# 64x64 tiles for a product of layer 1, and an earlier place for f, g and h of the second image in layer 2

## The chip, the cores and the metric

One core of one Trainium2 chip runs the whole kernel as a single program. The metric is the device time of that program in microseconds (us), the median of several executions. A trace by the hardware profiler gives one further execution in detail. Engines are named as in the profile: PE (TensorE matmuls; PEld are its weight loads), DVE (VectorE), ACT (ScalarE), POOL (GpSimd), SP (SyncE, which here issues DMAs).

## The reference

Four layers follow each other on x of shape (2, 512, 32, 32) in fp32, that is two images of 512 channels and 1024 pixels. Layer 0 is a deformable attention with a learned position bias and an MLP; the change does not touch it. The rest, cut to what matters:

```python
# layer 1: linear attention, 8 heads of d = 64 channels
K = conv1x1(X, Wq, bq); Q = conv1x1(X, Wk, bk); V = conv1x1(X, Wv, bv)   # each as (b, head, d, n)
M = einsum('bhmn,bhen->bhme', K, V)
Out = einsum('bhme,bhmn->bhen', M, Q)
Out = conv1x1(Out, Wo, bo) + X            # then a batch norm over both images, with gamma and beta
# layer 2: non-local attention, mid = 128
f = relu(bn_eval(conv1x1(x, wf, bf), ...)); g = relu(bn_eval(conv1x1(x, wg, bg), ...))
h = conv1x1(x, wh, bh)
attn = softmax(einsum('bcn,bcm->bnm', f, g) * mid ** -0.5)                 # 1024 x 1024 for each image
x = conv1x1(einsum('bnm,bcm->bcn', attn, h), wv, bv) + x
# layer 3: theta, phi and g have one channel each
y = softmax(theta[:, :, None] * phi[:, None, :]) @ g
x = sigmoid(se2(relu(se1(mean(x))))) * bn(W_w * y + W_b) + x
```

## The kernel before

The program is written in one function over tile pools. A scheduler orders the instructions of each engine by what they wait for, so the order in the text is not the order on the engine, except where an instruction is pinned (`keep_in_program_order`: in layer 0, and in `last` near the end). Channels lie on the 128 partitions in four blocks (`KC = 4`); an image is 1024 columns (`HW`). PSUM, where PE writes, has eight banks of 128x512 fp32 that the pools hand out; a pool's `bufs` says how many tiles of a tag can be open at once, and the next tile waits until the readers of an earlier one are done.

**Layer 1** never forms K, Q and V. It makes each image's Gram matrix G = X X' (L1357), and from it U = G Wv, M = Wq U (per head), R = M Wk and A = R Wo, all of 512x512, and at last the output from A and X. The products with 512 on every side go through `seven` (L1314 to L1334), a Strassen-like scheme: seven products of blocks instead of eight, each two matmuls of 128x256 columns on PE, with sums and differences on DVE. The eight heads of M lie on the diagonal: for block `o` the tile `M[b][:, o]` is 128x128, holds heads 2o and 2o+1 as two 64x64 blocks, and is zero beside them (the memset of L1441). The matmuls of M (L1447) already write 64 rows each; DVE adds the bias term to each block (L1457).

R is made per image and block by one 128x512 matmul (`prk`, L1472) into a one-bank PSUM tile of the pool `dpg` (tag "g", four buffers), which DVE (even blocks) or ACT (odd blocks) copies to SBUF (L1473). Beside it, small matmuls (`prb`, L1475) multiply M with the bias of Wk into the pool `dps` (tag "ps", four buffers). `weights_of(R[b])` then makes three working differences and one sum of R's blocks (S1, S2, S3, S4) on DVE, and `moving_of(wot)` those of the transposed Wo once. `seven` with R starts with a product that needs only R itself; its second product needs S2.

**Layers 2 and 3** run image by image from four functions. `l2_fg` (L1629) makes f and g: 16 matmuls (`pf2`) of 512 columns, evicted by four activations on ACT. `l2_h` (L1650) makes one of eight pixel blocks of h: four matmuls (`ph2`) of 128 columns, and one addition on DVE. `l2_attn` (L1662) goes through eight row blocks t: two matmuls into `pscore` (two banks, L1667), the row maximum on DVE (L1678), the exponential on ACT (L1681), reciprocal and scaling on DVE, eight transposes on PE (`pt2`, L1687) and two copies on ACT (L1688) into `at2`. Its argument `between` is called once for each t and puts other work between. `l2_out` (L1691) does 16 matmuls `pz` (L1696) that sum over all of `at2` and `ht`, eight matmuls `pr2` (L1707), and adds the result to x.

Layer 3 of image 0 is `l3_scores` (L1719): rows of theta, phi and g (`prow`, L1728), spread to all partitions (`pp3`, copied to `pg` in SBUF by ACT, L1750), extremes on DVE; it returns `part(t)` (L1774), one exponential of 128x1024 on ACT (L1776) and one weighting on DVE (L1784), for t = 0 to 7, on three buffers `e3`. `l3_out` (L1790) ends image 0 and stores it by four DMAs. For image 1 all of `l2_out` and layer 3 is in `last` (L1839), pinned in its order, and stores by eight DMAs.

The order of these is set at the end of the program (L2039 to L2058). Image 0's f, g, h, attention and `l2_out` use PSUM pools `fp1` (three one-bank buffers, tag "ps") and `fph` (one buffer, tag "h"), beside `fps` (two `pscore` of two banks each). Then these two pools close, and `fp2` (two buffers) and `gps` (one of two banks, tag "l3") open:

```python
nd, part = l3_scores(0, gp, gps)
fg = l2_fg(1, fp, ps)
ht = fp.tile([P, 8, MID], F32, name="ht")
for t in range(8):
    l2_h(1, t, ht, ps, "ps")
    if t % 2:
        part(t // 2)
at2 = l2_attn(1, fp, fps, ps, fg, lambda t: part(4 + t // 2) if t % 2 else None)
l3_out(0, gp, gps, nd)
```

So image 1's f, g and h come after image 0's `l3_scores`, four of the `part` go between the blocks of h, and four between the row blocks of the attention.

Of the kernel before, what the change touches and what calls it, by code (L numbers as in the profile page):

```python
# [10 lines left out]
F32 = mybir.dt.float32  # L11
# [5 lines left out]
P = 128  # L17
B, C, H, W = 2, 512, 32, 32
HW = H * W
NT = B * HW  # L20
KC = C // P
TK = 8
DH = 64
# [4 lines left out]
MID = C // 4  # L28
# [44 lines left out]
def conv_seq(  # L73
# [22 lines left out]
    nc = tc.nc  # L96
# [40 lines left out]
    with ExitStack() as ctx_l0:  # L137
# [264 lines left out]
        with tc.tile_pool(name="a", bufs=1) as a, tc.tile_pool(name="apk", bufs=1, space=PSUM) as apk, tc.tile_pool(  # L402
            name="apc", bufs=1, space=PSUM
# [13 lines left out]
            for t in (0, 2, 1, 3):  # L417
                b, half = divmod(t, 2)
# [136 lines left out]
            for i, (ky, kx) in enumerate(taps_pe):  # L555
# [4 lines left out]
                        lhsT=diag[:, i, :],  # L560
                        rhs=qg[:, ch.g, yi, r, c_, xi],
                        start=(i == 0),
                        stop=(i == len(taps_pe) - 1),
# [72 lines left out]
        with tc.tile_pool(name="hid", bufs=3) as hid, tc.tile_pool(name="sm", bufs=1) as sm, tc.tile_pool(name="hps", bufs=2, space=PSUM) as hps, tc.tile_pool(  # L636
            name="sps", bufs=1, space=PSUM
# [451 lines left out]
        for t in range(NT // 512):  # L1089
            ts_ = slice(t * 512, (t + 1) * 512)  # L1090
            for o in range(KC):
                po = mh.tile([P, 512], F32, name="po")
                for k in range(KC):
                    nc.tensor.matmul(  # L1094
                        po,
                        lhsT=(vwo, wo)[t // 2][:, k, o * P : (o + 1) * P],
                        rhs=q[:, k, ts_],
                        start=(k == 0),
                        stop=(k == KC - 1),
# [46 lines left out]
    with ctx_w:  # L1146
        with tc.tile_pool(name="mo", bufs=2, space=PSUM) as mo, tc.tile_pool(name="m", bufs=3) as m, tc.tile_pool(name="mv", bufs=1) as mv:
# [22 lines left out]
            hs = {}  # L1170
# [106 lines left out]
    with tc.tile_pool(name="d", bufs=2) as d, tc.tile_pool(name="dpg", bufs=4, space=PSUM) as dpg, tc.tile_pool(  # L1277
        name="dps", bufs=4, space=PSUM
    ) as dps:
        both = range(B)  # L1280
        wq, wv, wk, wot, won = (lw[:, i] for i in range(5))
# [3 lines left out]
        G, U, M, R, A, bias1 = {}, {}, {}, {}, {}, {}  # L1285
# [55 lines left out]
        for b in both:  # L1341
# [3 lines left out]
            for t in range(8):  # L1345
# [10 lines left out]
                for i in range(KC):  # L1356
                    nc.tensor.matmul(  # L1357
                        pgs[i],
                        lhsT=xt[:, i * P : (i + 1) * P],
# [78 lines left out]
        for b in both:  # L1438
# [4 lines left out]
            for o in range(KC):  # L1443
# [11 lines left out]
                for h in range(2):  # L1455
# [7 lines left out]
                        ALU.add,  # L1463
                    )
        rblocks, prbs = {}, {}
        for b in both:
            R[b] = d.tile([P, KC, C], F32, name="R", tag="G")
            prb = prbs[b] = dps.tile([P, C], F32, name="prb", tag="ps")
            for o in range(KC):
                mo_ = M[b][:, o].rearrange("p h e -> p (h e)")  # L1470
                pr = dpg.tile([P, C], F32, name="prk", tag="g")
                nc.tensor.matmul(pr, lhsT=mo_, rhs=wk[:, o, :], start=True, stop=True)  # L1472
                (nc.vector.tensor_copy, nc.scalar.copy)[o % 2](R[b][:, o, :], pr)  # L1473

                nc.tensor.matmul(  # L1475
                    prb[:, o * P : (o + 1) * P],
                    lhsT=v("L1_conv_bk", o).to_broadcast([P, P]),
                    rhs=mo_,
                    start=True,
                    stop=True,  # L1480
                )
            rblocks[b], steps = weights_of(R[b])
            for step in steps:
                step()
            if b == 0:
                wotblocks, steps = moving_of(wot)
                for step in steps:
                    step()
# [140 lines left out]
    def l2_fg(b, fp, ps):  # L1629
        fg = fp.tile([P, 2, HW], F32, name="fg")  # L1630
        for i, half in ((0, 0), (0, 1), (1, 0), (1, 1)):
            pf = ps.tile([P, 512], F32, name="pf2", tag="ps")
            for j, k in enumerate((0, 2, 3, 1)):
                nc.tensor.matmul(
                    pf,
                    lhsT=l2w[:, k, i, :],
                    rhs=x[:, k, b * HW + half * 512 : b * HW + (half + 1) * 512],
                    start=(j == 0),
                    stop=(j == KC - 1),
                )  # L1640
            nc.scalar.activation(
                fg[:, i, half * 512 : (half + 1) * 512],
                pf,
                AF.Relu,
                bias=l2s[:, 1, 1:2] if i else l2f[:, 1:2],
                scale=l2s[:, 0, 1:2] if i else l2f[:, 0:1],
            )
        return fg

    def l2_h(b, t, ht, ps, tag):  # L1650
        ph = ps.tile([P, MID], F32, name="ph2", tag=tag)
        for k in range(KC):
            nc.tensor.matmul(
                ph,
                lhsT=x[:, k, b * HW + t * P : b * HW + (t + 1) * P],
                rhs=l2w[:, k, 2, :],
                start=(k == 0),
                stop=(k == KC - 1),
            )
        nc.vector.tensor_tensor(ht[:, t, :], ph, rowb[:, C : C + MID], ALU.add)  # L1660

    def l2_attn(b, fp, fps, ps, fg, between=None):  # L1662
        at2 = fp.tile([P, 8, HW], F32, name="at2", bufs=1)
        for t in range(8):
            pscore = fps.tile([P, 2, 512], F32, name="pscore")
            for half in range(2):
                nc.tensor.matmul(  # L1667
                    pscore[:, half, :],
                    lhsT=fg[:, 0, t * P : (t + 1) * P],
                    rhs=fg[:, 1, half * 512 : (half + 1) * 512],  # L1670
                    start=True,
                    stop=True,
                )
            if between is not None:
                between(t)
            psf = pscore.rearrange("p a n -> p (a n)")
            nm = fp.tile([P, 1], F32, name="nm")
            nc.vector.tensor_reduce(nm, psf, AX.X, ALU.max, negate=True)  # L1678
            e2 = fp.tile([P, HW], F32, name="e2")
            den = fp.tile([P, 1], F32, name="den2")  # L1680
            nc.scalar.activation(e2, psf, AF.Exp, bias=nm, accum_out=den)  # L1681
            nc.vector.reciprocal(den, den)
            nc.vector.tensor_scalar(e2, e2, den, None, ALU.mult)
            for mg in range(2):
                pt = ps.tile([P, 4, P], F32, name="pt2", tag="ps")
                for i in range(4):
                    nc.tensor.transpose(pt[:, i, :], e2[:, (mg * 4 + i) * P : (mg * 4 + i + 1) * P], ident)  # L1687
                nc.scalar.copy(at2[:, mg * 4 : mg * 4 + 4, t * P : (t + 1) * P], pt)  # L1688
        return at2

    def l2_out(b, fp, ps, at2, ht):  # L1691
        z = fp.tile([P, HW], F32, name="z")
        for half in range(2):
            pz = ps.tile([P, 512], F32, name="pz", tag="ps")
            for t in range(8):
                nc.tensor.matmul(  # L1696
                    pz,
                    lhsT=ht[:, t, :],
                    rhs=at2[:, t, half * 512 : (half + 1) * 512],
                    start=(t == 0),  # L1700
                    stop=(t == 7),
                )
            nc.scalar.copy(z[:, half * 512 : (half + 1) * 512], pz)
        for half in range(2):
            for o in range(KC):
                pr = ps.tile([P, 512], F32, name="pr2", tag="ps")
                nc.tensor.matmul(  # L1707
                    pr,
                    lhsT=l2wv[:, o * P : (o + 1) * P],
                    rhs=z[:, half * 512 : (half + 1) * 512],  # L1710
                    start=True,
                    stop=True,
                )
                xs = x[:, o, b * HW + half * 512 : b * HW + (half + 1) * 512]
                nc.vector.scalar_tensor_tensor(
                    xs, pr, v("L2_conv_bv", o), xs, ALU.add, ALU.add, accum_out=xavg[:, o, b, half : half + 1]
                )
# [319 lines left out]
    with tc.tile_pool(name="f", bufs=2) as fp, tc.tile_pool(name="g", bufs=1) as gp:  # L2037
        with tc.tile_pool(name="fps", bufs=2, space=PSUM) as fps:
            with tc.tile_pool(name="fp1", bufs=3, space=PSUM) as ps, tc.tile_pool(  # L2039
                name="fph", bufs=1, space=PSUM  # L2040
            ) as psh:
                fg = l2_fg(0, fp, ps)
                ht = fp.tile([P, 8, MID], F32, name="ht")
                at2 = l2_attn(0, fp, fps, ps, fg, lambda t: l2_h(0, t, ht, psh, "h"))
                l2_out(0, fp, ps, at2, ht)
            with tc.tile_pool(name="fp2", bufs=2, space=PSUM) as ps:
                with tc.tile_pool(name="gps", bufs=1, space=PSUM) as gps:
                    nd, part = l3_scores(0, gp, gps)
                    fg = l2_fg(1, fp, ps)
                    ht = fp.tile([P, 8, MID], F32, name="ht")  # L2050
                    for t in range(8):
                        l2_h(1, t, ht, ps, "ps")
                        if t % 2:
                            part(t // 2)
                    at2 = l2_attn(1, fp, fps, ps, fg, lambda t: part(4 + t // 2) if t % 2 else None)
                    l3_out(0, gp, gps, nd)
                with tc.tile_pool(name="gpl", bufs=2, space=PSUM) as gps:
                    last(1, fp, gp, fps, ps, gps, at2, ht)  # L2058
# [126 lines left out]
```

## Time and profile before

| what | us |
|---|---|
| median of 3 executions (lowest to highest) | 2659.73 (2659.29 to 2660.62) |
| the profiled execution | 2659.86 |
| its span, first to last instruction | 2658.1 |

The mean TensorE clock granted over the profiled execution was 0.995 of full speed. By stages of that execution:

| stage | from, to | length | PE busy | DVE busy | ACT busy | PE clock |
|---|---|---|---|---|---|---|
| layer 0, position bias | 0 to 1789 | 1789 | 1771.89 | 1741.04 | 1331.63 | 1.00 |
| layer 0, rest of it and first part of the MLP | 1789 to 2090 | 301 | 300.14 | 185.46 | 98.81 | 1.00 |
| layer 0, MLP | 2090 to 2320 | 230 | 229.98 | 118.89 | 30.83 | 1.00 |
| layer 1, G and U | 2320 to 2395.1 | 75.1 | 72.91 | 39.95 | 8.87 | 1.00 |
| layer 1, M and R | 2395.1 to 2409.1 | 14.0 | shown below | | | |
| layer 1, A | 2409.1 to 2433.9 | 24.8 | shown below | | | |
| layer 1, output | 2433.9 to 2481.8 | 47.9 | 47.90 | 38.39 | 3.92 | 1.00 |
| norm, layer 2 of image 0: f, g, h, attention | 2481.8 to 2530.1 | 48.3 | 44.02 | 25.04 | 23.33 | 0.98 |
| `l2_out` of image 0 | 2530.1 to 2551.5 | 21.4 | 21.40 | 5.23 | 1.76 | 0.96 |
| layer 3 of image 0, layer 2 of image 1 | 2551.5 to 2606.1 | 54.6 | shown below | | | |
| `last`: rest of image 1 | 2606.1 to 2658.1 | 52.0 | 34.10 | 30.25 | 17.60 | 0.80 |

The three rows left open are printed with the prediction. Busy times are sums over the instructions in a stage. A PE that is busy for the whole of a stage says that no other engine held it up there, not that each matmul ran at its best. The last column is the mean clock that the throttle granted to PE in the stage. In the lines below, "PE L1687 MATMUL pt<-cst,e 128*128 128x128 f32 x8" is eight matmuls of line 1687 that write `pt` (names are cut short), on a tile of 128*128 of the array, with an output of 128 partitions x 128 columns; the numbers ahead are start and length in us, and a bracket behind gives the idle time before and what ended it.

### The profile page before, as it was taken

Reading aid. Unit: us, or ns where it says so; the run is one execution under the profiler, and the core shown is the slowest. Engines: PE = TensorE matmul, PEld = TensorE weight load, DVE = VectorE, ACT = ScalarE, POOL = GpSimd, SP = SyncE. Lnnn points to the kernel's source line nnn. Section 1 sums busy time; section 2 is a strip of 40 time slices with the busy share of each in tenths; the row PEclk is TensorE's granted clock in tenths of the full one; section 3 lists DMA queues with packets and bytes.
Section 4 is the critical chain, followed back from the end, with each engine's and each line's share of the span. In section 5 each row is a group of like instructions: output and inputs, shape, how many; then the busy total and the mean of one; then the engine's idle time right before and its main releaser. Section 6 shows DMA issues by size and latency. Waiting matters only on the chain.

```text
span 2658.1 us, 48935 instructions
## 1 busy us (share of the span) xinstructions
PE 2613.7 (98%) x19658; PEld 970.8 (37%) x19658; DVE 2249.6 (85%) x2036; ACT 1557.1 (59%) x2138; POOL 889.2 (33%) x1049
## 2 busy tenths in 40 slices
PE   8999999999999999999999999999999999999997
PEld 4332323233332333333233333323444444476544
DVE  8999999999999999999999999999554444648645
ACT  6776787777678777767867777777221111011334
POOL 2444444444444454444444445444200000000001
PEclk9999999999999999999999999999999999999998
DMA  6888888888888888888989898888410000010001
GB/s 219 162 180 172 161 162 160 170 161 179 169 161 159 162 173 159 181 169 162 176 164 174 159 183 171 157 176 162 97 31 24 16 24 24 27 53 1 0 1 64
DMA packets 114003, 339.23 MB, mean 128 GB/s; under 512 B 22736, under 2 KB 32464, under 8 KB 112496
## 3 DMA queue, kind: packets, MB, share of 16 engines
q0 software_dynamic: 77824, 251.72, 53.0%
q1 hardware_dynamic: 35520, 84.10, 9.6%
q8 instruction: 155, 2.54, 0.4%
q14 instruction: 72, 0.59, 0.1%
q10 hardware_dynamic: 432, 0.28, 0.0%
HBM read 63.12 MB, written 4.46 MB: 25 GB/s over the span
## 4 chain that ended last, share of the span: by engine, by line
PE 90%; DVE 4%; ACT 3%; issue 2%; DMA 1%; POOL 0%; DVEq 0%; ACTq 0%
PE ph L658 61%; PE A L1159 4%; PE D L1159 4%; PE C L1159 4%; PE po L1094 2%; PE B L1159 2%; PE pg L1357 1%; DVE h L390 1%; ACT r L667 1%; DVE r L673 1%; PE pscore L1667 1%; DMA r<-r 1%; PE psim L701 1%; PE pz L1696 1%; PE pt L1687 1%
## 5 line engine op out<-in xcount | busy, mean ns | idle before, releaser
L658 PE MATMUL ph<-h,w2a 128*32 128x512 f32 x16384 | 1772.1, 592 | 10.3 <-ACT r L667 7.5
L667 ACT ACTIVATE r<-ph,sb 128x1024 f32<-128x1024 f32 x1024 | 1141.6, 1115 | 467.8 <-PE ph L658 444.4
L390 DVE CUSTOM_DVE_ANT_1 h<-tab 128x2048 f32<-128x2048 f32 x512 | 1170.5, 2286 | 19.2 <-PE ph L658 16.4
L658 PEld LDWEIGHTS ph<-h,w2a 128*32 128x32 f32 x16384 | 520.9, 109 | 1238.4 <-issue 768.9
L673 DVE SCALAR_TENSOR_TENSOR r<-r,rel,r 128x1024 f32<-128x1024 f32 x512 | 655.1, 1279 | 25.9 <-ACT r L667 24.5
L681 POOL DMA_DIRECT2D r<-r x512 | 474.7, 1142 | 170.8 <-DMA r<-r 160.7
L676 POOL DMA_DIRECT2D r<-r x256 | 234.4, 916 | 733.2 <-DVE r L673 621.9
L692 POOL DMA_DIRECT2D xs<-r x256 | 320.3, 1251 | 103.6 <-DMA xs<-r 97.8
L1441 POOL MEMSET M<- 128x512 f32 x2 | 1.0, 525 | 428.7 <-PE pt L1348 428.7
L176 ACT ACTIVATE tab<-tab,vec 128x256 f32<-128x256 f32 x252 | 137.6, 546 | 0.0
L1952 POOL TENSOR_TENSOR x<-x,aff 128x512 f32<-128x512 f32 x7 | 7.0, 1036 | 318.0 <-ACT e L1917 318.0
L1199 ACT COPY u<-A 128x512 f32<-128x512 f32 x16 | 9.4, 586 | 146.8 <-PE A L1159 146.8
L1178 ACT ACTIVATE h<-h,vec 128x512 f32<-128x512 f32 x32 | 23.1, 721 | 113.5 <-DVE h L1181 113.5
L1181 DVE TENSOR_TENSOR h<-C,u 128x512 f32<-128x512 f32 x32 | 22.1, 691 | 48.5 <-PE C L1159 48.2
L1159 PE MATMUL A<-xn,w 128*128 128x512 f32 x128 | 60.3, 593 | 0.8 <-DVE x L1101 0.8
L1159 PE MATMUL C<-hT,w 128*128 128x512 f32 x128 | 60.3, 592 | 0.0
L1159 PE MATMUL A<-h,w 128*128 128x512 f32 x128 | 60.1, 592 | 0.0
L1219 DVE TENSOR_TENSOR x<-D,x 128x512 f32<-128x512 f32 x32 | 22.1, 692 | 26.0 <-PE D L1159 26.0
L1219 DVE TENSOR_TENSOR x<-C,x 128x512 f32<-128x512 f32 x32 | 22.1, 691 | 24.8 <-PE C L1159 24.8
L892 ACT ACTIVATE e<-e,den 128x64 f32<-128x64 f32 x128 | 42.3, 341 | 0.5 <-DVE den L888 0.5
L878 ACT ACTIVATE e<-psm,mx 128x64 f32<-128x64 f32 x128 | 39.4, 314 | 2.4 <-DVE mx L873 2.3
L1357 PE MATMUL pg<-xt 128*128 128x512 f32 (+3 forms) x128 | 36.4, 439 | 1.4 <-ACT xt L1355 1.1
(411 smaller groups left out, 1918.1 us busy)
## 6 DMA issues: line engine op xcount, KB each, us to landing
r<-r POOLq DMA_DIRECT2D x256, 512.0 KB, 5.0
r<-r POOLq DMA_DIRECT2D x256, 256.0 KB, 5.9
r<-r POOLq DMA_DIRECT2D x256, 128.0 KB, 4.7
tab<-fd SPq DMA_DIRECT2D x63, 512.0 KB, 6.4
xs<-r SPq DMA_DIRECT2D x256, 64.0 KB, 2.7
xs<-r POOLq DMA_DIRECT2D x256, 64.0 KB, 5.5
lw<-in_l_w_dram SPq DMA_DIRECT2D x5, 1024.0 KB, 9.0
x<-in_x_pos_dram SPq DMA_DIRECT2D x4, 1024.0 KB, 17.9
```

The lines of the kernel that those rows point to most:

```text
L176: return nc.scalar.activation(tf, tf if src is None else src[:, :, ax, :], AF.Identity, bias=0.0 if ax == 0 else v("L0_conv_cpb_b1"), scal ...
L390: nc.vector._custom_dve(TENSOR_ADD_SAT, out=h1, in0=columns.unsqueeze(1).to_broadcast([P, 32, 2, 32]), in1=rows_.unsqueeze(3).to_broadcast ...
L658: nc.tensor.matmul(ph[t * 32 : (t + 1) * 32, i, :], lhsT=w2a[:, o], rhs=h1s[2 * p + i][:, half * 16 : (half + 1) * 16, h, :], start=True, ...
L667: pin(nc.scalar.activation(r, ph, AF.Relu, bias=sb3[:, o, 1:2]))
L673: pin(nc.vector.scalar_tensor_tensor(r0, r1, rel[:, i : i + 1], r0, ALU.mult, ALU.add))
L676: pin(nc.gpsimd.dma_start(rs[p, 0], rs.pop((p, 2)), accum_op=ALU.add))
L681: pin(nc.gpsimd.dma_start(r[0 :: 2 * step], r[step :: 2 * step], accum_op=ALU.add))
L692: pin(nc.gpsimd.dma_start(xs_[t][d::8], rs.pop((p, 0))[4::8], accum_op=ALU.add))
L1094: nc.tensor.matmul(po, lhsT=(vwo, wo)[t // 2][:, k, o * P : (o + 1) * P], rhs=q[:, k, ts_], start=(k == 0), stop=(k == KC - 1),)
L1159: nc.tensor.matmul(banks[bank], lhsT=a[an][k], rhs=b_[bn_][k], start=(i < 4 and k == 0), stop=(k == n - 1), skip_group_check=True,)
L1219: nc.vector.tensor_tensor(to, t, to, ALU.add)
L1357: nc.tensor.matmul(pgs[i], lhsT=xt[:, i * P : (i + 1) * P], rhs=xt[:, i * P :], start=(t == 0), stop=(t == 7),)
```

## The change

It has two parts, both of order and tiling. What is computed stays.

**R.** The loop over images and blocks becomes a loop over blocks that serves both images. For each block `o` four matmuls of 64 rows and 512 columns take the four 64x64 blocks of M (image 0 and 1, head 2o and 2o+1) with the matching 64 rows of Wk. Each contracts over 64 partitions (`hs`) and writes 64 partitions of PSUM, so each uses one quarter of the array: for image 0 rows and columns of the same half, for image 1 the output goes to the other half (`half(h ^ b)`), which makes the four quarters different. Image 0's tile is copied as before by one copy, on DVE for even and ACT for odd blocks. Image 1's halves stand exchanged in PSUM and are copied by two copies of 64 partitions each, one on ACT (h = 0) and one on DVE (h = 1). The bias matmuls `prb` move behind this loop and read the same M.

**f, g and h of image 1.** `l2_fg(1)` moves ahead of `l2_out(0)`, and all eight `l2_h(1)` behind it, inside image 0's PSUM pools; the h take the one-buffer tag "h". `l3_scores(0)` comes after them. All eight `part` of image 0's layer 3 are handed to image 1's attention as its `between`, one for each row block, where before there were four between the h and four in the attention.

```diff
         rblocks, prbs = {}, {}
+
+        def half(h):
+            return slice(h * DH, (h + 1) * DH)
+
         for b in both:
             R[b] = d.tile([P, KC, C], F32, name="R", tag="G")
+        for o in range(KC):
+            prk = [dpg.tile([P, C], F32, name="prk", tag="g") for b in both]
+            for b, h in ((0, 0), (0, 1), (1, 0), (1, 1)):
+                hs = half(h)
+                nc.tensor.matmul(
+                    prk[b][half(h ^ b)], lhsT=M[b][hs, o, h, :], rhs=wk[hs, o, :], start=True, stop=True
+                )
+            (nc.vector.tensor_copy, nc.scalar.copy)[o % 2](R[0][:, o, :], prk[0])
+            for h in range(2):
+                (nc.scalar.copy, nc.vector.tensor_copy)[h](R[1][half(h), o, :], prk[1][half(h ^ 1)])
+        for b in both:
             prb = prbs[b] = dps.tile([P, C], F32, name="prb", tag="ps")
             for o in range(KC):
-                mo_ = M[b][:, o].rearrange("p h e -> p (h e)")
-                pr = dpg.tile([P, C], F32, name="prk", tag="g")
-                nc.tensor.matmul(pr, lhsT=mo_, rhs=wk[:, o, :], start=True, stop=True)
-                (nc.vector.tensor_copy, nc.scalar.copy)[o % 2](R[b][:, o, :], pr)
-
                 nc.tensor.matmul(
                     prb[:, o * P : (o + 1) * P],
                     lhsT=v("L1_conv_bk", o).to_broadcast([P, P]),
-                    rhs=mo_,
+                    rhs=M[b][:, o].rearrange("p h e -> p (h e)"),
                     start=True,
                     stop=True,
                 )
...
                 at2 = l2_attn(0, fp, fps, ps, fg, lambda t: l2_h(0, t, ht, psh, "h"))
+                fg = l2_fg(1, fp, ps)
                 l2_out(0, fp, ps, at2, ht)
+                ht = fp.tile([P, 8, MID], F32, name="ht")
+                for t in range(8):
+                    l2_h(1, t, ht, psh, "h")
             with tc.tile_pool(name="fp2", bufs=2, space=PSUM) as ps:
                 with tc.tile_pool(name="gps", bufs=1, space=PSUM) as gps:
                     nd, part = l3_scores(0, gp, gps)
-                    fg = l2_fg(1, fp, ps)
-                    ht = fp.tile([P, 8, MID], F32, name="ht")
-                    for t in range(8):
-                        l2_h(1, t, ht, ps, "ps")
-                        if t % 2:
-                            part(t // 2)
-                    at2 = l2_attn(1, fp, fps, ps, fg, lambda t: part(4 + t // 2) if t % 2 else None)
+                    at2 = l2_attn(1, fp, fps, ps, fg, part)
                     l3_out(0, gp, gps, nd)
                 with tc.tile_pool(name="gpl", bufs=2, space=PSUM) as gps:
                     last(1, fp, gp, fps, ps, gps, at2, ht)
```

In the order that the scheduler gives the changed program, the first seven of image 1's 32 h matmuls stand on PE between image 0's last scores and its last transposes, then f and g, then `pz` and `pr2` of image 0, then the other h matmuls among image 1's scores. On ACT, the first five of image 1's eight attention exponentials come before the first of `part`, the sixth behind six of `part`, the seventh behind seven, and the last behind all eight.

## The prediction

> **What bounds the kernel now.** First the chain of waits that ended last:
>
> ```profile
> PE 90%; DVE 4%; ACT 3%; issue 2%; DMA 1%; POOL 0%; DVEq 0%; ACTq 0%
> ```
>
> TensorE's own work is the chain. So the question is whether PE gets less to do, or idles less, where the change acts. Next, stages by window (columns: length, then busy time and instructions of PE, PEld, DVE, ACT, POOL; PE clock; DMA):
>
> ```profile
> 2395.10:2409.10 14.00, 13.72 (x161) 8.86 (x161) 12.93 (x29) 2.25 (x4) 0.00 (x0) 1.00 0.01 1
> 2409.10:2433.90 24.80, 24.75 (x115) 21.34 (x115) 19.11 (x48) 4.15 (x10) 0.00 (x0) 1.00 0.00 1
> 2551.50:2606.10 54.60, 52.86 (x257) 31.18 (x257) 33.33 (x72) 33.97 (x59) 0.00 (x0) 1.00 0.00 1
> ```
>
> The first row holds M and the products R, the second their use in `seven`, the third runs from the end of `l2_out(0)` to the start of `last`. PE is full in all three. But DVE is busy 12.93 of 14.00 in the first, so a PE saving there meets DVE at once.
>
> Third, the two things about PE itself that decide the prices: a 64x64 group that the kernel already runs, and its idle gap at the end of image 0's attention.
>
> ```profile
> 15.97 1.09 PE L468 MATMUL pq<-xn,qws 64*64 64x512 f32 x8
> 16.99 0.66 PE L257 MATMUL pf<-acc,offw 128*128 128x64 f32 x4
> ...
> 2528.33 1.94 PE L1687 MATMUL pt<-cst,e 128*128 128x128 f32 x8 [2.74 <-DVE e L1683]
> 2530.06 14.71 PE L1696 MATMUL pz<-at,ht 128*128 128x512 f32 x32
> ```
> ```profile
> 2525.70:2528.30 2.60, 0.00 (x0) 0.00 (x1) 1.37 (x4) 1.21 (x2) 0.00 (x0) 0.99 0.00 0
> 2528.30:2531.70 3.40, 3.37 (x10) 2.44 (x11) 0.00 (x0) 1.17 (x2) 0.00 (x0) 0.50 0.02 5
> 2531.70:2533.40 1.70, 1.70 (x5) 0.76 (x4) 0.00 (x0) 0.00 (x0) 0.00 (x0) 1.00 0.00 0
> ```
>
> The trace counts two passes for each fp32 matmul. Passes of 512 columns elsewhere start 0.429 us apart, so a matmul costs 0.858. Four matmuls on four 64x64 tiles took 16.99 - 15.97 = 1.02 us, not 3.43: they do run together. The gap of 2.74 us is followed by 3.4 us at clock 0.50, which loses 1.7 us of work.
>
> **Part 1, R by 64x64 tiles.** Before: 8 matmuls x 0.858 = 6.86 us. After: 16 matmuls of half size; if all went four at a time, 4 x 0.858 = 3.43. In the changed program's order, though, PE takes each image's M between them: one matmul alone, then three together, again one alone, and eleven in three rounds. That is 6 x 0.858 = 5.15, so PE saves at most 1.72.
>
> The price is on the copies:
>
> ```profile
> L1473 DVE COPY R<-prk x4: 684/688/692, 2399.8 to 2409.3; 128x512 f32<-128x512 f32 x4
> L1473 ACT COPY R<-prk x4: 586/586/587, 2401.3 to 2409.1; 128x512 f32<-128x512 f32 x4
> ```
>
> Time goes by columns, so I give a half-height copy the same cost (between half of it and all of it; no row shows 64x512 on these). Each engine then has six copies instead of four: DVE +2 x 0.60 (0.60 being its spacing between such operations in a row). ACT is idle and hides its two. DVE from the first M (2395.98) to the second difference S2 of image 0 must do 16 M x 0.295 + two differences of the weights 1.2 + six copies 3.6 + two differences of x 2.28 + S1 and S2 1.2 = 13.0, so 2409.0 if it never waits; my walk through its waits (M waits for PE, the second half copies for ACT's, since both write one tile) ends at 2409.8. PE's second product of `seven`, which needs S2, started at 2410.00 before. So 0.2 to 1.0 is gained there; further on, PE waits for `uv22` on DVE, whose queue is 1.2 longer, and keeps 0.2 to 1.0. I take -0.4. Bounds: -1.72 (PE alone) and +1.2 (the two copies whole).
>
> [...]
>
> **Part 2a, the lead.** Image 1's first seven h matmuls and then its f and g come before `l2_out(0)`. The h fill the gap of 2.74 (one DVE add, 0.28, delays the last scaling, so the transposes start 2528.6 instead of 2528.33), and with PE active there I expect no half clock: eight transposes x 0.107 end at 2529.45. Before, the 16 `pz` matmuls (13.73) ended at 2544.61, as if begun at full clock at 2530.88. The lead is 1.43. The 16 f and g matmuls, 13.73, now stand in front, and the end of `l2_out(0)` on PE comes 13.73 - 1.43 = 12.3 later: 2563.8 instead of 2551.5.
>
> [...]
>
> **Part 2b, the stage that follows.** It took 2606.15 - 2551.47 = 54.68 and must shrink to 42.4 to break even. Its PE work falls by 13.73 + 1.5. What else it holds:
>
> ```profile
> L1776 ACT ACTIVATE e<-pg,nm,th 128x1024 f32<-128x1024 f32 x8 | 9.8, 1232 | 2.1 <-DVE nm L1770 1.4 <-DVE e L1784 0.6
> L1678 DVE TENSOR_REDUCE nm<-pscore 128x1 f32<-128x1024 f32 x8 | 9.7, 1214 | 2.3 <-PE pscore L1667 2.3
> L1784 DVE SCALAR_TENSOR_TENSOR e<-e,pg 128x1024 f32<-128x1024 f32 x8 | 9.4, 1224 | 5.5 <-ACT pg L1750 5.1 <-ACT e L1776 0.5
> L1681 ACT ACTIVATE e<-pscore,nm 128x1024 f32<-128x1024 f32 x8 | 9.0, 1125 | 4.9 <-DVE nm L1678 4.9
> L1688 ACT COPY at<-pt 128x512 f32<-128x512 f32 x16 | 8.7, 589 | 6.4 <-PE pt L1687 6.3
> L1660 DVE TENSOR_TENSOR ht<-ph,rowb 128x128 f32<-128x128 f32 x8 | 2.2, 287 | 1.8 <-PE ph L1653 1.8
> ```
>
> Before, layer 3's eight exponentials ran while PE did f, g and h. That cover is gone: now they compete with the attention's exponentials. I count from the end of `pr` on PE, through the new order. (a) h has one PSUM buffer, so each h waits for DVE's add of the last; six of them, the `prow` groups (PSUM free only after the h) and the scores put the third row maximum at 14.0. (b) Steps of maximum 1.26, exponential 1.2, reciprocal and scaling 1.1, with layer 3's rows, `pg` copies and extremes between, bring the start of the fifth exponential to 23.9. (c) From there ACT is in line: three attention exponentials x 1.18, eight of layer 3 x 1.235, two `pg` 1.34, two copies 1.08 = 15.85, until 39.75. PE has nothing from 29.6 to 36.2, since its score bank waits for the sixth exponential. (d) The last weighting 1.15, maximum 1.26, exponential 1.25, reciprocal to scaling 1.1, transposes 1.1: `pz` of `last` at 45.7. The gap of 6.6 must halve the clock as 2.74 did; scores and transposes then go at half speed up to some 41, and the eighth score comes about 0.6 late, transposes and copies behind it 0.3: 46.6.
>
> So part 2 is 12.3 + 46.6 - 54.68 = +4.2. Bounds of the stage: 37.7 (before's PE busy time less what moved, no waiting) and 50.8 (half clock to the end). The output DMAs, 4 + 8, stay in order and wait for the same things.
>
> **Sum.** The profiled execution took 2659.86 (span 2658.1, 1.8 around it), 0.13 above the median 2659.73. 2659.86 - 0.4 + 4.2 = 2663.7; by the median 2663.6. The rest of the order is as before.
>
> **Rivals.**
> A, the forecast: 2663.6, range 2660.5 to 2667.
> B, slower: the clock does not come back after the gap. Place: PE from 36.2 on. Price: the last `py` (1.72) and transposes (0.86) double, and the first 3.4 us of `pz` give 1.7: stage 50.8, 2667.9. For: in `last` the clock of this trace falls and stays at 0.50. Against: after 2531.7 one busy stretch of 3.4 us restored it. It decides over 0.2% (5.3 us) once the stage passes 48.2.
> C, faster: the stage runs as full as before, 37.7, and part 1 gives its 1.0: 2654.0. For: ACT 33.97 and DVE 33.33 leave room in 37.7. Against: the order above, six layer 3 exponentials ahead of the sixth attention one.
> D, hidden: stage about 42.5, part 1 -0.4: 2659.3.
> E, the tiles do not overlap: 16 x 0.858 instead of 5.15, +8.6: 2672. The `pq` row is against it.
>
> **Chances.** A 0.55 (0.37 within 0.2%, 0.18 above), B 0.26, D 0.12, C 0.05, E 0.02. Bounds of +-0.2%, about what a measurement of this kernel can tell from no change, are 2654.4 and 2665.0. Faster 0.04 (most of C), same 0.50 (A's 0.37, D, a rest of C), slower 0.46 (A's 0.18, B, E). The range 2658.8 to 2668.8 leaves out C, some of D, the top of B and E.
>
> **What would show it.** `prk` on 64*64 tiles, eight passes or so in 1 us; `seven` on R starting under 1 us earlier; no 0.50 clock near 2530 and PE full from there; `pr` of image 0 ending 12 later; then a PE hole of some 6 us with ACT full of L1786, and clock 0.50 behind it. Wrong would be: `seven` starting over 1.5 earlier (half copies cheap), or the stage under 42 or over 48.

## The result, and the profile after

The changed kernel takes 2666.13 us (median of 12 executions, 2665.30 to 2667.23), the kernel before 2659.67 (12 executions, 2658.06 to 2661.32). The ratio is 1.0024 with a 95% interval of 1.0017 to 1.0032: slower by 4.5 to 8.5 us. The forecast was 2663.6 with a range of 2658.8 to 2668.8.

The stages can be measured better than the whole. Up to layer 1 both kernels run the same instructions, but the moment at which the first matmul of M starts lies anywhere from 2394.8 to 2398.5 us in the profiles below, whatever the kernel. Counted from that start, a stage that isn't touched repeats to 0.02 us between executions (38.53 or 38.54 to layer 1's output in ten profiles with the old R). So I count from there. The end of `pr2` is taken as 0.43 after the start of its last pass, the spacing of such passes:

| us from the first matmul of M to | before | changed | difference |
|---|---|---|---|
| second product of `seven` with R | 14.83 | 15.73 | +0.90 |
| first matmul of layer 1's output | 38.54 | 39.32 | +0.78 |
| end of image 0's `pr2` | 156.31 | 169.35 | +13.04 |
| first `pz` of `last` | 210.98 | 216.96 | +5.98 |
| first `pyl` of `last` | 247.74 | 253.46 | +5.72 |

The loss is the sum of three terms: 0.8 in R, 12.3 by f and g ahead of `l2_out(0)` (net of what the filled gap saves), and only 7.1 of that comes back in the stage behind it (47.6 instead of 54.7).

The view of stages by window, of the changed kernel (length, then busy time and instructions of PE, PEld, DVE, ACT and POOL, then PE clock and DMA):

```profile
2395.10:2408.90 13.80, 13.35 (x177) 7.47 (x177) 12.45 (x28) 3.99 (x7) 0.00 (x0) 1.00 0.01 2
2408.90:2434.50 25.60, 24.66 (x115) 20.89 (x114) 20.93 (x51) 3.57 (x9) 0.00 (x0) 1.00 0.00 1
2564.50:2612.10 47.60, 40.86 (x211) 25.07 (x209) 34.15 (x72) 30.24 (x55) 0.00 (x0) 0.93 0.00 1
2594.90:2600.70 5.80, 0.06 (x2) 0.00 (x0) 5.80 (x12) 5.80 (x12) 0.00 (x0) 0.92 0.00 0
2600.70:2604.10 3.40, 3.32 (x8) 1.77 (x9) 3.33 (x9) 3.40 (x7) 0.00 (x0) 0.50 0.00 0
```

The third row answers to the stage of 54.60 before: PE was busy for all but 1.7 of it and is now idle for 6.7. In the fourth row PE does next to nothing (0.06) while ACT and DVE are busy without a break; in the fifth the clock is 0.50. PE's timeline of the changed kernel has the gap at the end of image 0's attention, now filled, and the new hole:

```profile
2526.97 1.16 PE L1663 MATMUL ph<-l2w,x 128*128 128x128 f32 x8 [0.62 <-DVE ht L1670]
2528.51 0.94 PE L1663 MATMUL ph<-l2w,x 128*128 128x128 f32 x6 [0.38 <-DVE ht L1670]
2529.28 1.04 PE L1697 MATMUL pt<-cst,e 128*128 128x128 f32 x8
2530.16 13.90 PE L1644 MATMUL pf<-x,l2w 128*128 128x512 f32 x32
...
2594.55 0.41 PE L1811 MATMUL pse<-avg,se1w 128*32 128x1 f32 x8
2600.72 2.07 PE L1677 MATMUL pscore<-fg 128*128 128x512 f32 x2 [5.76 <-ACT e L1691]
2602.86 1.94 PE L1697 MATMUL pt<-cst,e 128*128 128x128 f32 x8
2604.59 1.92 PE L1677 MATMUL pscore<-fg 128*128 128x512 f32 x2
...
2612.11 14.00 PE L1879 MATMUL pz<-at,ht 128*128 128x512 f32 x32 [0.24 <-ACT at L1698]
```

The eight transposes take 1.04 and not 1.94: full clock. The hole of 5.76 ends when an exponential of the attention (L1691) frees the score bank. Groups of that stage:

```profile
L1677 PE MATMUL pscore<-fg 128*128 128x512 f32 x32 | 17.9, 663 | 5.8 <-ACT e L1691 5.8
L1786 ACT ACTIVATE e<-pg,nm,th 128x1024 f32<-128x1024 f32 x8 | 9.9, 1241 | 0.0
L1698 ACT COPY at<-pt 128x512 f32<-128x512 f32 x16 | 9.0, 584 | 8.1 <-PE pt L1697 8.1
L1691 ACT ACTIVATE e<-pscore,nm 128x1024 f32<-128x1024 f32 x8 | 8.9, 1117 | 13.5 <-DVE nm L1688 13.5
```

Durations are as before (1241 against 1232 ns, 1117 against 1125). What changed is the waiting: layer 3's exponentials never wait now, and those of the attention wait 13.5 instead of 4.9, 9.5 of it at the stage's start.

### The profile page after: what moved, and what is told of

Read it like the earlier page. It is cut to its first block, busy times and chain, and to the rows that moved or that the text cites. A ratio compares the mean times of both kernels' runs of the same rounds, so it can differ in the third digit from the quotient of the medians.

```text
span 2663.8 us, 48972 instructions
## 1 busy us (share of the span) xinstructions
PE 2615.2 (98%) x19674; PEld 969.5 (36%) x19674; DVE 2250.6 (84%) x2038; ACT 1557.7 (58%) x2140; POOL 888.6 (33%) x1049
## 4 chain that ended last, share of the span: by engine, by line
PE 90%; DVE 4%; ACT 3%; issue 2%; DMA 1%; POOL 0%; DVEq 0%; ACTq 0%; SPq 0%
PE ph L658 61%; PE A L1159 4%; PE D L1159 4%; PE C L1159 4%; PE B L1159 2%; PE po L1094 2%; PE pg L1357 1%; DVE h L390 1%; ACT r L667 1%; PE pscore L1677 1%; DVE r L673 1%; PE pf L1644 1%; PE psim L701 1%; DMA r<-r 1%; PE prD L1326 1%
## 5 line engine op out<-in xcount | busy, mean ns | idle before, releaser
L658 PE MATMUL ph<-h,w2a 128*32 128x512 f32 x16384 | 1772.1, 592 | 10.2 <-ACT r L667 7.5
L692 POOL DMA_DIRECT2D xs<-r x256 | 313.2, 1223 | 111.8 <-DMA xs<-r 97.3
L1677 PE MATMUL pscore<-fg 128*128 128x512 f32 x64 | 33.5, 629 | 5.8 <-ACT e L1691 5.8
```

The costliest lines, as they stand in the source:

```text
L658: nc.tensor.matmul(ph[t * 32 : (t + 1) * 32, i, :], lhsT=w2a[:, o], rhs=h1s[2 * p + i][:, half * 16 : (half + 1) * 16, h, :], start=True, ...
L692: pin(nc.gpsimd.dma_start(xs_[t][d::8], rs.pop((p, 0))[4::8], accum_op=ALU.add))
L1677: nc.tensor.matmul(pscore[:, half, :], lhsT=fg[:, 0, t * P : (t + 1) * P], rhs=fg[:, 1, half * 512 : (half + 1) * 512], start=True, stop=True,
```

## The experiments

All are counted as in the table above; "stage" is from the end of image 0's `pr2` to the first `pz` of `last`. Ratios are to the kernel before, with a 95% interval.

| run | to layer 1's output | to end of `pr2` | stage | to `pz` of `last` | time, ratio |
|---|---|---|---|---|---|
| before | 38.54 | 156.31 | 54.67 | 210.98 | 2659.67 |
| changed | 39.32 | 169.35 | 47.61 | 216.96 | 2666.13, 1.0024 |
| R alone | 39.33 | 155.45 | 54.67 | 210.12 | 2660.07, 1.0002 (0.9993 to 1.0011) |
| R, copies on ACT | 38.26 | 156.09 | 54.66 | 210.75 | 2660.75, 1.0003 (0.9995 to 1.0012) |
| f, g, h alone | 38.54 | 168.58 | 47.53 | 216.11 | 2665.34, 1.0022 (1.0013 to 1.0031) |
| h in the gap | 38.54 | 155.07 | 52.88 | 207.95 | 2657.08, 0.9989 (0.9980 to 0.9998) |
| parts later | 38.53 | 168.56 | 49.74 | 218.30 | 2668.04, 1.0027 (1.0017 to 1.0036) |
| hole filled | 38.53 | 168.55 | 49.23 | 217.78 | 2667.27, 1.0026 (1.0017 to 1.0035) |
| before again | 38.53 | 156.12 | 54.67 | 210.79 | 2662.36, one execution |
| h in gap, copies on ACT | 38.25 | 154.76 | 52.88 | 207.64 | 2657.68, 0.9986 (0.9978 to 0.9995) |
| f, g alone | 38.54 | 169.70 | 47.08 | 216.78 | 2665.75, 1.0025 (1.0014 to 1.0036) |
| h alone | 38.53 | 154.83 | 59.59 | 214.42 | 2664.60, 1.0021 (1.0011 to 1.0030) |
| half the parts | 38.53 | 168.55 | 45.13 | 213.68 | 2665.62, one execution |
| both holes filled | 38.53 | 168.54 | 48.15 | 216.69 | 2665.80, one execution |

### R alone

The first part of the change's diff on the kernel before.

> Only the R part of the change; f, g and h of image 1 stay where they were. Theory (two more copies on DVE and their waits for ACT put S2 back, and PE waits for it): the second product of `seven` starts 0.9 later than the 2410.00 of before, the layer's output starts 0.8 later, and the kernel takes 2660.4 us, 0.8 more than before. Rival 1 (the forecast: DVE is about where it was and PE gains): 2659.2, 0.4 less. Rival 2 (it costs only together with the other part): no difference.

To layer 1's output it takes 39.33, 0.79 more than before: the theory's 0.8. The whole kernel shows no difference (2660.07 against 2660.14), with an interval wide enough to hide 0.8. In the profile the end of `pr2` comes at 155.45, earlier than before's 156.31: the half clock behind the gap was absent in this execution, which is worth 1.65 (0.79 + 156.31 - 155.45). PE's timeline of this run:

```profile
2412.04 1.13 PE L1326 MATMUL prB<-t,s 128*128 128x256 f32 x4 [0.94 <-DVE s L1295]
...
2530.24 1.06 PE L1697 MATMUL pt<-cst,e 128*128 128x128 f32 x8 [2.74 <-DVE e L1693]
2531.14 13.90 PE L1706 MATMUL pz<-at,ht 128*128 128x512 f32 x32
```

The wait for S2 is there (0.94). So is the gap, 2.74 as before, but the transposes behind it take 1.06.

### R with the half copies on ACT

```diff
-                (nc.scalar.copy, nc.vector.tensor_copy)[h](R[1][half(h), o, :], prk[1][half(h ^ 1)])
+                nc.scalar.copy(R[1][half(h), o, :], prk[1][half(h ^ 1)])
```

> As the run with R alone, but all eight half copies of image 1 are on ACT, so DVE has two copies of R instead of six (before: four). Theory (DVE is the limit): PE gets through the products of R without waiting for S2, the second product of `seven` starts near 2409.4, the layer's output starts 0.6 earlier than before, and the kernel takes 2659.0 us. Rival (the changes of tiling on PE eat the gain): as with R alone, PE itself is late, 2660.4.

PE's timeline of this run:

```profile
2403.72 4.02 PE L1476 MATMUL prk<-lw,M 64*64 64x512 f32 x22
2407.67 2.05 PE L1485 MATMUL prb<-M,vec 128*128 128x128 f32 x16
2409.56 1.03 PE L1326 MATMUL prA<-lw,R 128*128 128x256 f32 x4
2410.42 1.06 PE L1326 MATMUL prB<-t,s 128*128 128x256 f32 x4
```

PE doesn't wait for S2 any more; the second product starts 14.08 after M's start, 0.75 earlier than before. Same matmuls, same changes of tiling, so DVE's copies were the cost, not PE. PE itself gained little: the last eleven products (22 passes, the first line) took 3.95, not the 2.57 of three rounds. Only 0.28 of the 0.75 is left at layer 1's output, under the expected 0.6. In the whole time that can't be seen.

### f, g and h alone

The second part of the diff on the kernel before.

> Only the second part of the change; R as before. Theory (the parts are independent; the image 0 end moves back 12.3, the stage behind shrinks from 54.7 to 47.6, and the last stage gains 0.3): 2664.6 us, 4.9 more than before, with the same PE hole of about 5.8 us behind the scores and clock 0.50 after it. Rival (the cost comes from both parts together): 2660 to 2662, or 2666.

The end of `pr2` is 12.27 later, the stage 47.53, `pz` of `last` 5.13 later, and the time 5.2 more. The hole of 5.76 is there, with 6.8 us of clock 0.50 behind it, as the theory said. The parts add: 0.78 + 5.13 = 5.91, against 5.98 for both.

### h in the gap

```diff
+                early = fp.tile([P, 8, MID], F32, name="ht")
+                for t in range(2):
+                    l2_h(1, t, early, psh, "h")
                 l2_out(0, fp, ps, at2, ht)
...
-                    ht = fp.tile([P, 8, MID], F32, name="ht")
+                    ht = early
                     for t in range(8):
-                        l2_h(1, t, ht, ps, "ps")
+                        if t > 1:
+                            l2_h(1, t, ht, ps, "ps")
```

> Before, with only the first two pixel blocks of image 1's h moved ahead of image 0's `l2_out`, so that seven of their eight matmul groups lie in the gap of 2.74 us; f, g, the other h and layer 3 stay. Theory (the gap halves the clock, and the stage behind is full on PE): 1.4 from the clock and 1.5 to 1.7 from the work taken out of the later stage, 2656.6 us, 3.0 less than before, no clock of 0.50 near 2530. Rival 1 (the half clock comes from something else than the gap): 1.6 less, 2658.0. Rival 2 (the later stage is held by ACT and DVE): 1.4 less at most, 2658.2.

`pz` of `last` comes 3.03 earlier, the expected 3.0: 1.24 up to `pr2`, 1.79 in the stage. The median is 3.1 lower. Against an execution in which the gap costs no clock, as in R alone, 1.4 of the 3.03 would be left. Two of the eight blocks are all that the gap needs, and layer 3 isn't delayed.

### Parts later

On top of f, g and h alone:

```diff
-                    at2 = l2_attn(1, fp, fps, ps, fg, part)
+                    at2 = l2_attn(1, fp, fps, ps, fg, lambda t: part(t - 5) if t > 4 else None)
+                    for t in range(3, 8):
+                        part(t)
```

> Second part alone (as in the run of f, g and h alone), but layer 3's eight `part` are handed in five row blocks later, so that on ACT the sixth attention exponential stands behind two of them and not behind six. Theory (the score bank waits for an exponential that ACT reaches late): the PE hole of 5.8 us shrinks to about 1, the clock stays at 1.00, the stage from the end of `pr2` to `pz` of `last` falls from 47.5 to 43, and the kernel takes 0.5 to 1 us more than before instead of 5. Rival (ACT and DVE have that much to do in any order): the hole only moves, the stage stays at 46 to 48, 4 to 5 us more than before.

PE's timeline of this run:

```profile
2596.50 1.98 PE L1667 MATMUL pscore<-fg 128*128 128x512 f32 x4 [0.88 <-ACT e L1681]
2598.79 1.06 PE L1687 MATMUL pt<-cst,e 128*128 128x128 f32 x8 [0.31 <-DVE e L1683]
2602.94 1.06 PE L1687 MATMUL pt<-cst,e 128*128 128x128 f32 x8 [3.08 <-DVE e L1683]
...
2611.37 3.71 PE L1821 MATMUL py<-cst,y 128*128 128x128 f32 x16 [0.49 <-DVE y L1793]
2614.91 13.90 PE L1869 MATMUL pz<-at,ht 128*128 128x512 f32 x32
```

The hole shrank to 0.88 as the theory said, and the stage grew by 2.2. The theory falls, and the rival was right in kind (it expected a stage of 46 to 48, measured 49.7; 4 to 5 us more time than before, measured 7.4). Now layer 3 ends last: its last exponential ends at 2608.77, `py` needs the sums of all eight, and `pz` stands behind `py` on PE. The holes moved (3.08) and the clock was 0.50 for 10.2 us. In both orders ACT has one run of work from layer 3's first exponential on: in f, g and h alone the last attention rows stand late in it, here layer 3 does.

### The hole filled, and both holes filled

On top of f, g and h alone, first 24 matmuls whose results nobody reads, behind the small `pse` matmuls of layer 3 that PE does just before the hole, then also 7 ahead of the transposes of each of the last two row blocks:

```diff
+        for _ in range(24):
+            nc.tensor.matmul(pse[:, 0, 256:384], lhsT=ident, rhs=ident, start=True, stop=True)
         mid = gp.tile([SE, 1], F32, name="mid")
...
                 pt = ps.tile([P, 4, P], F32, name="pt2", tag="ps")
+                for _ in range(7 if (b, mg) == (1, 0) and t > 5 else 0):
+                    nc.tensor.matmul(pt[:, 0, :], lhsT=ident, rhs=ident, start=True, stop=True)
```

> Second part alone, with 24 matmuls of 128x128 that nobody reads put on PE where the hole is (24 x 0.215 = 5.2 us of the 5.8); ACT and DVE keep their order. Theory (the hole costs twice, by the wait and by the half clock behind it): no clock of 0.50 there, scores and transposes behind it at full speed, `pz` of `last` 1.2 to 1.6 us earlier. Rival (ACT sets the pace behind the hole and the half clock costs nothing): `pz` of `last` moves by less than 0.3.

> As the run with the hole filled, with 7 more unread matmuls of 128x128 ahead of the transposes of each of the last two row blocks, so that PE is also busy in the shorter waits behind the hole. Theory (any step of 3.41 us in which PE is idle for most of the time halves the clock in the next, so the half clock of the first filled run was moved, not avoided): no clock of 0.50 between 2590 and 2615, the stage from the end of `pr2` to `pz` of `last` 45 to 46, so 1.5 to 2.5 less than the 47.5 of the second part alone. Rival (the half clock costs nothing, the waits for ACT set the time): 47.5 or more.

With the hole alone filled, the clock fell one wait later, from 2605.8 to 2612.6, and `pz` came 1.67 later. Neither theory had that. This is the wait, from PE's timeline of that run:

```profile
2605.53 1.69 PE L1687 MATMUL pt<-cst,e 128*128 128x128 f32 x8 [1.94 <-DVE e L1683]
```

With both filled the clock stayed at 1.00, and the stage is 48.15, not the 45 to 46 expected: by its number the rival (47.5 or more) was right. PE's timeline of the run with both filled:

```profile
2600.47 1.99 PE L1667 MATMUL pscore<-fg 128*128 128x512 f32 x4 [0.20 <-ACT e L1681]
...
2608.09 1.83 PE L1687 MATMUL pt<-cst 128*128 128x128 f32 x14
2609.75 1.04 PE L1689 MATMUL pt<-cst,e 128*128 128x128 f32 x8
2610.62 1.95 PE L1825 MATMUL py<-cst,y 128*128 128x128 f32 x16
2612.41 13.90 PE L1873 MATMUL pz<-at,ht 128*128 128x512 f32 x32
```

The last attention exponential starts 209.1 after M's start instead of 212.1 (in f, g and h alone). But the unread matmuls themselves stand for 1.66 in front of the last transposes, and the scheduler put all of `py` behind them, where it isn't hidden. So what the half clock alone costs at `pz` isn't isolated. Both runs agree that filling PE doesn't repair the stage.

### Before again

The kernel before, unchanged.

> The kernel before, unchanged, for a second look at its clock. Theory (the clock is set in fixed steps of 3.41 us, by what PE did in the step before, and the steps lie differently against the program in each execution): all changes of the clock are whole multiples of 3.41 us apart, and the gap of 2.74 us is followed by 3.41 us at 0.50 or by nothing at all, either with its 1.6 us of PE time. Rival (the clock falls 2.7 us into any gap): it is 0.50 again from the first transpose after the gap, at the same place as in the first profile.

The clock fell at 2530.46, 2.35 us into the gap (before: 2.68), and rose 3.4 later; the third change comes at 2639.7, 32 steps of 3.41 after the first. In the run with R on ACT, the same gap of 2.74 ended at 2529.22 and the clock fell at 2530.06, 0.8 behind it; in R alone it didn't fall at all. So the rival, a fixed delay from the start of a gap, is out.

### h in the gap and copies on ACT

Both edits above with the tiles of R: the version made from what the runs showed.

> R by 64x64 tiles with all half copies on ACT, and two of image 1's h blocks in the gap before image 0's `l2_out`; f, g and the rest stay as before. Theory (the two gains lie in different stages and add): start of M to the layer's output 0.3 shorter than before, gap filled and clock at 1.00, later stage shorter by the work moved, in all 3.3 us less than a profile of before in which the gap halves the clock, 1.7 less than one in which it doesn't: 2657 us. Rival (what is saved in R is waited for on DVE later): as with h in the gap alone.

`pz` of `last` comes 3.34 earlier than before, where 0.28 and 3.03 make 3.31. The time is 2657.68 against 2660.67, ratio 0.9986 (0.9978 to 0.9995): below the kernel before, and by more below the changed one. That R adds to the h is seen in the stages only (0.31); the medians of the two versions don't tell them apart.

### f and g alone, and h alone

Each half of the second part by itself: `fg = l2_fg(1, fp, ps)` ahead of `l2_out(0)` with all else as before, and the eight `l2_h(1)` behind `l2_out(0)` with f and g as before:

```diff
                 l2_out(0, fp, ps, at2, ht)
+                ht = fp.tile([P, 8, MID], F32, name="ht")
+                for t in range(8):
+                    l2_h(1, t, ht, psh, "h")
...
                     fg = l2_fg(1, fp, ps)
-                    ht = fp.tile([P, 8, MID], F32, name="ht")
-                    for t in range(8):
-                        l2_h(1, t, ht, ps, "ps")
-                        if t % 2:
-                            part(t // 2)
+                    for t in range(4):
+                        part(t)
```

> Of the second part only f and g of image 1 move ahead of image 0's `l2_out`; its h and layer 3's `part` stay as before. Theory (f and g were the PE work under which ACT did layer 3's exponentials; h is too short for it): the end of `pr2` of image 0 comes 13.7 us later from the start of M, the stage behind it shrinks by only 9 to 11.5 us, the gap before the last transposes stays, and `pz` of `last` comes 2 to 5 us later than before. Rival (moving h is what costs, since h then has one PSUM buffer): no later than 0.5.

> Of the second part only the eight h of image 1 move, with one PSUM buffer as in the change; f and g stay behind layer 3's scores, and four `part` come before the attention, four in it. Theory (f and g remain as cover, seven h groups fill the gap): no clock of 0.50 near the gap, `pz` of `last` 2.5 to 3 us earlier than before from the start of M, about 2657.2. Rival (the one buffer for h costs): `pz` of `last` no earlier than before.

f and g alone cost 5.80 at `pz` of `last`, above the expected 2 to 5, with the stage 7.6 shorter for 13.4 put in front. PE then has a hole of 4.41 while ACT does layer 3's exponentials:

```profile
2592.73 2.08 PE L1667 MATMUL pscore<-fg 128*128 128x512 f32 x2 [4.41 <-ACT e L1681]
```

For h alone the theory was wrong and the rival right by its number: 3.44 later instead of 2.5 to 3 earlier. It gains 1.48 up to `pr2` by the gap and loses 4.92 in the stage. PE's timeline of h alone:

```profile
2549.58 0.39 PE L1653 MATMUL ph<-l2w,x 128*128 128x128 f32 x2
2550.60 1.13 PE L1634 MATMUL pf<-x,l2w 128*128 128x512 f32 x2 [0.63 <-DVE x L1715]
...
2562.16 1.07 PE L1728 MATMUL prow<-x,w3x 128*32 128x512 f32 x8
...
2585.00 3.78 PE L1667 MATMUL pscore<-fg 128*128 128x512 f32 x4 [4.16 <-ACT e L1681]
```

The remaining h alternate with f and g, one at a time through their one buffer, and layer 3's rows (`prow`) come behind them, 12.6 us after the end of `pr2`. Before they came after 1.0 (2552.49 against 2551.48), and with h in the gap, too. PE is idle for only 0.63 of that stretch, so it is the order that puts them back. Whether a second buffer for h would let them come earlier wasn't tried.

### Half the parts

On top of f, g and h alone:

```diff
+                    at2 = l2_attn(1, fp, fps, ps, fg, lambda t: part(t) if t < 4 else None)
+                    nc.vector.tensor_copy(nd[:, :, 4:8], nd[:, :, 0:4])
```

> Second part alone, with the last four of image 0's eight `part` left out (their sums are copied from the first four, so half of that layer's exponentials and weightings are missing). Theory (behind `pr2` ACT does one unbroken run of work, and its length sets the stage): four exponentials of 1.235 us less, and a shorter PE hole: the stage from the end of `pr2` to `pz` of `last` falls from 47.5 to 42 or 43, `pz` of `last` 4.5 to 6 us earlier than with all eight. Rival (each row's chain from score to transposes sets the pace): 2 us earlier at most.

The stage falls by 2.40, between the two expectations. PE's timeline of this run:

```profile
2600.79 2.07 PE L1667 MATMUL pscore<-fg 128*128 128x512 f32 x2 [3.31 <-ACT e L1681]
...
2612.16 14.00 PE L1869 MATMUL pz<-at,ht 128*128 128x512 f32 x32 [0.24 <-ACT at L1688]
```

The hole is 3.31 instead of 5.76: the two exponentials missing ahead of the sixth attention exponential count in full (2 x 1.235 = 2.47). The two missing behind it count for nothing: from the score after the hole to `pz` it is 11.37 here and 11.39 in the changed kernel. So ACT's queue sets the time up to the end of the hole, and layer 3's work left on ACT behind it does not.

## Why the prediction came out as it did

**Part 1 had the wrong sign.** Forecast -0.4, measured +0.78, inside the bounds of -1.72 to +1.2. The step that failed first is DVE's walk, which ended at 2409.8 and said that it meets PE's second product in time. DVE's timeline of the changed kernel:

```profile
2405.28 0.69 DVE L1481 COPY R<-prk 64x512 f32<-64x512 f32 x1 [0.51 <-ACT R L1481]
2406.00 0.69 DVE L1479 COPY R<-prk 128x512 f32<-128x512 f32 x1
2406.72 1.23 DVE L1545 TENSOR_TENSOR lw<-x,lw 128x1024 f32<-128x1024 f32 x1
2407.98 0.69 DVE L1481 COPY R<-prk 64x512 f32<-64x512 f32 x1
2408.70 0.69 DVE L1294 TENSOR_TENSOR s<-R 128x512 f32<-128x512 f32 x1
2409.42 0.68 DVE L1481 COPY R<-prk 64x512 f32<-64x512 f32 x1
2410.14 0.69 DVE L1295 TENSOR_TENSOR s<-s,R 128x512 f32<-128x512 f32 x1
```

S2 (L1295) ends at 2410.82, 14.87 after the start of DVE's first M (2395.95). The prediction's terms sum to 13.0, and its walk allowed 0.8 for waits. DVE waited for only 0.51 (the first line, for ACT's half, as foreseen). The rest, about 1.4, is spacing: each of these operations starts 0.72 after the one before (1.26 behind the wide one), where I took 0.60 (1.14). The six copies alone take 4.3 instead of 3.6. That a half-height copy costs what a whole one does was right (684 against 691 ns on DVE, 582 against 586 on ACT). Before, S2 was ready at 2408.19 and PE's second product at 2410.00 didn't wait for it; now that product waits 0.94. The lines are DVE's of before and PE's of the changed kernel:

```profile
2407.51 0.68 DVE L1295 TENSOR_TENSOR s<-s,R 128x512 f32<-128x512 f32 x1
```
```profile
2410.88 1.13 PE L1326 MATMUL prB<-t,s 128*128 128x256 f32 x4 [0.94 <-DVE s L1295]
```

The second term that failed is PE's saving of 1.72, from 6.86 to 5.15. PE comes to the tiled products in four visits. A visit takes 1.0 for one matmul or three (2396.28 to 2397.27, 2398.36 to 2399.37), as the `pq` row said for four. The eleven of the last visit stand in four groups of four, three, two and two, not in three rounds; with copies on ACT, where PE waits for no copy, they took 3.95. The four visits of that run sum to 6.96, against 7.2 for the eight products of before, counted in the same way (from the start of a product to that of the next other matmul). So the tiles save 0.2 on PE, and in the changed kernel PE reached `seven` 0.20 earlier (13.77 after M's start instead of 13.97). Why the eleven fall into four groups stays open. Each of the first three visits is about 0.14 longer (0.99, 1.01 and 1.00) than the 0.858 that the prediction's 5.15 counts for it; no run isolates what takes that time. The run with copies on ACT has the same four visits and no loss, so they weren't what decided.

**Part 2a held.** The lead was forecast at 1.43 and the end of `pr2` at +12.3; less part 1 it is 13.04 - 0.78 = 12.26. The transposes start 0.19 later by h's addition (forecast 0.27) and run at full clock. But the 1.65 of half clock that the fill saves (1.47 in before again, 1.71 in R on ACT) isn't lost in every execution with the gap: R alone had the gap and kept its clock. The gap of 2.74 was followed by half clock in four of the five profiles that have it. The clock changed in steps of 3.41 that lie differently against the program in each profile (last section): in R alone the gap falls on two of them, in the other four most of it on one, and that would explain why the same gap costs nothing or 1.65.

**Part 2b: the mechanism held, its tail was 1.0 short.** The hole was forecast from 29.6 to 36.2 after `pr2` and lay from 30.5 to 36.2 (2600.72 - 2564.50). Behind it I had 10.4 to `pz`; it took 11.4. The half clock lasted two steps, 2599.8 to 2606.6, not "up to some 41" (2605.5), so the eighth row's maximum waited until 2606.54, 0.69 after DVE was free. Then two copies on ACT held its exponential for 0.3, and `py` on PE held the last transposes for 0.56 (the last scaling ended at 2610.27). The latter two weren't in the walk.

**Sum.** -0.4 + 4.2 became 0.78 + 5.20 = 5.98 at `pz`, and 0.26 came back in `last`. The likeliest case was right about the mechanism and put too near to no change by 1.2 in part 1 and by 1.0 in part 2b. Rival B (clock stays half, stage 50.8) didn't happen: it came back after 6.8 us. C and D needed a stage of 37.7 or 42.5; the one other order of `part` that was tried made it longer (49.74). E is out: one after the other the eleven products of the last visit would take 9.4 (11 x 0.858), not 3.95.

**What the stage really lacks.** "That cover is gone" was right, and the single runs show two causes. Layer 3's first exponential started 11.15 us after `pr2` before, and starts 25.40 after it now; the two lines are from ACT's timelines, of before (`pr2` ended at 2551.48) and of the changed kernel (2564.50):

```profile
2562.63 1.24 ACT L1776 ACTIVATE e<-pg,nm,th 128x1024 f32<-128x1024 f32 x1 [1.44 <-DVE nm L1770]
```
```profile
2589.90 1.25 ACT L1786 ACTIVATE e<-pg,nm,th 128x1024 f32<-128x1024 f32 x1
```

With f and g alone it starts after 12.0, and the kernel still loses 5.80: f and g are the PE work beside which ACT did the eight. With h alone f and g are there, but the start is 23.05 after `pr2`, and the kernel loses 3.44. Either loss is enough. With h in the gap neither occurs (the start is 11.15 after `pr2`, as before), and it gains 3.03.

Open are the price of the half clock behind the hole, and an order of the moved version in which `pz` doesn't stand behind `py`; neither was isolated.

## What to carry to other kernels

Work that PE can do at any time is worth most beside another engine's long run; before it is moved into a gap, ask what it covers where it stands, and move only as much as the gap holds: two blocks of h gained 3.0 us (1.4 where the gap would have cost no clock), all of f, g and h lost 5.1. When a matmul gets cheaper by tiling, count the evictions: halves that need a copy each cost whole copies (on DVE 684 ns for 64 partitions, 691 for 128), on the engine that already sets the pace. And look at what comes behind moved work in its queue: six more blocks of h ahead of layer 3's rows put a whole chain back by 12 us.

## What the runs showed of the hardware

The clock changed only in whole steps of 3.41 us: in ten profiles the changes lie 1, 2, 3, 12, 13, 17, 18, 20, 32 or 34 such steps from the first in the same profile, within 0.05 of a step, and the grid lies differently against the program in each. The falls go with how busy PE was within one step of that grid. From 2300 us on, the fourteen profiles have 1376 such steps at full clock. In 25 of them PE was busy for 1.43 us or less of the 3.41, by the profile, and each of these was followed by half clock; in the other 1351 it was busy for 1.7 or more, and none was. So the same gap of 2.74 us was followed by half clock in four of five profiles (before, before again, R on ACT, f and g alone: 0.73, 1.06, 0.84 and 1.40 busy in the step) and by none in R alone, where two steps share it (2.13 and 1.95 busy).

What brings the clock back isn't settled. It came back after half-clock steps with PE busy for 2.7 (f and g alone) and 3.0 (before again), but not after one with 2.4 (the changed kernel), one with 2.8 (half the parts), nor after one in which PE was busy throughout (the hole filled, 2605.80 to 2609.21). So the busy time of the profile alone doesn't decide it.
